# One recurrent block on one core: last batch's x fetched early, seven rows in round one, z fetched two blocks later, last values summed on TensorE, last stores in pieces

## The chip, the cores and the metric

The kernel runs on one core of one Trainium2 chip, in float32 throughout. The metric is the device time of one execution in microseconds (us). The engines are called PE (TensorE, matmuls), DVE (VectorE), ACT (ScalarE), POOL (GpSimd) and SP (SyncE, which here only issues DMAs). Each runs its own list of instructions in order and waits for the others through semaphores. DMAs are issued from a queue of SP, POOL or ACT.

## What is computed

For x of 8 batches of 1024 tokens of 256 features:

```
xn = layernorm(x)
s  = attention(xn)          # per token: 4 heads against 4 heads, softmax over heads
                            # heads and tokens swapped and reshaped, then Wo
z  = xn + experts(xn)       # Sinkhorn routing over 8 experts, the best 2 of each token
out = x + s * silu(z)
```

An expert is relu(x wg) * (x wp), times wo, for 512 hidden features. The attention is among the heads of one token, so its score is a 4x4 matrix for each token. The swap before Wo means that a row of s takes its parts from several tokens of the same batch: the s of a batch is complete only when all its tokens are.

## The kernel before

**Blocks.** A block (`blk`) is 4 tiles of 128 tokens, half a batch; there are 16. Normalised rows go to `xn_d` in DRAM, transposed ones to `xT_d`; `z_d` begins as a copy of `xn_d`.

**Attention as a generator.** `attention` (L866) yields after each small step, so that other loops can mix its steps with their own. For each tile `score` computes queries and keys (PE, L702) and their dot products (DVE, L715). Some blocks later `values_of` (L836) runs `value` (L766) for each tile. It computes the values times Wo, `u`, with four strips of 32 columns side by side on PE (`pu`, L785), adds a bias on DVE (L792), and sums over heads with the softmax weights `sc`. There are two forms of that sum. With `beside_experts[0]` set, DVE weighs (16 operations into `w`, L804 and L808), and PE puts the four head rows in place (`po_s`, L812, with an identity strip). Otherwise DVE builds a weighted identity, `mixer` (one operation, L773), and PE does the whole sum (`po_s`, L817). The weighing form yields once more. ACT copies the result to `s_out` (L824). After four tiles `values_of` stores `s_out` to `s_d` in the swapped order (L848) and marks the batch `attended`. For the last batch it keeps `s_out` in SBUF (`attended_rows`), since its two blocks can be finished in the swapped order of rows.

**Experts.** Of 71 possible groups of 256 (token, expert) pairs, the first 68 (`SURE`) always run; three more stand behind a branch (L1203) that this input doesn't take. A group is gathered, transposed (`ptr_g`, L933), multiplied by wg and wp (`pg`, `pp`, L945) and by wo (`po`, L961), scaled on ACT (L971) and added into `z_d` by two indirect DMAs of POOL (L974). The loop at L1192 takes an attention step after each of six steps of an expert. SP fetches the weights two groups ahead (L919).

**Finish.** When the last group has been added, the tail begins. For each block, `fetch_sums` (L1037) loads z from `z_d` into one of `SUMS` = 9 buffers, `fetch_other` (L1010) loads x and s into one of `AHEAD` = 8 pairs of buffers, and `finish` (L1052) does silu on ACT (L1059), the product with s and the sum with x on DVE (L1060, L1061), and the store from POOL (L1066; for the last batch four stores in swapped rows, L1064). Three pairs are loaded early, in the loop of experts (steps 96, 192 and 288), five when the scores are done and their buffers are free. The nine z loads come with the tail. In the tail each `finish` has four steps of attention ahead of it and the fetches of later blocks behind it: x and s of block `blk + 8`, then z of `blk + 9`. A fetch waits until the buffer's previous user is done: x and s for the sum of an earlier block on DVE, z for an earlier block's store. On SP's queue all later fetches stand behind a waiting one.

**Order.** The program's framework places instructions on each engine by its own estimate of times, so the order on PE, DVE and ACT isn't the order of the program text; DMAs of one queue stay close to it.

Of the kernel before, what the change touches and what calls it, by code (L numbers as in the profile page):

```python
# [9 lines left out]
F32 = mybir.dt.float32  # L10
AF = mybir.ActivationFunctionType
ALU = mybir.AluOpType
# [4 lines left out]
P = 128  # L17
# [13 lines left out]
def recurrent_kernel(  # L31
# [20 lines left out]
    nc = tc.nc  # L52
    B, S, D = x.shape
    H = phase.shape[0]
# [5 lines left out]
    J = P // R  # L60
    NT = S // P
    T = B * NT
    TB = 4
# [7 lines left out]
    SURE = N - 3  # L71
# [18 lines left out]
    def rows_of(a, b: int, first: int):  # L90

        return a[b * S + first * P : b * S + (first + TB) * P].rearrange(
            "(t p) d -> p t d", p=P
        )

    def block_of(a, blk: int):

        return a[blk * TB * P : (blk + 1) * TB * P].rearrange("(p t) d -> p (t d)", t=TB)
# [6 lines left out]
    n = 1  # L105
# [58 lines left out]
    s_d = dram.tile([B * S, D], F32, name="s_d")  # L164
# [601 lines left out]
    def value(tile_no: int, xT, t: int, sc, s_out):  # L766


        weigh = beside_experts[0]
        if not weigh:  # L770
            mixer = att.tile([P, H, H, J], F32, tag="mixer", name=f"mixer_{tile_no}")
            full = [P, H, H, J]
            nc.vector.tensor_tensor(  # L773
                mixer,
                onerow.unsqueeze(1).unsqueeze(1).to_broadcast(full),
                sc[:, t].rearrange("p (h g) -> p g h", h=H).unsqueeze(3).to_broadcast(full),
                ALU.mult,
            )
        u = att.tile([P, H * D], F32, tag="u", name=f"u_{tile_no}")
        for half in range(2):  # L780
            cols = slice(half * 512, (half + 1) * 512)
            pu = ps_tr.tile([P, 512], F32, tag="tr", name=f"pu_{tile_no}_{half}")
            for k in range(KD):
                for i in range(R):
                    nc.tensor.matmul(  # L785
                        pu[i * J : (i + 1) * J, :],
                        xT[:, t, k, i * J : (i + 1) * J],
                        w_vo[:, k, i, cols],
                        start=(k == 0),
                        stop=(k == KD - 1),  # L790
                    )
            nc.vector.tensor_tensor(  # L792
                u[:, cols], pu, b_vo.rearrange("p g d -> p (g d)")[:, cols], ALU.add
            )
            yield
        po = ps_out.tile([P, 512], F32, tag="out", name=f"po_s_{tile_no}")
        if weigh:

            w = att.tile([P, H, D], F32, tag="w", name=f"w_{tile_no}", bufs=1)
            for h in range(H):  # L800
                for g in range(H):
                    part, share = u[:, g * D : (g + 1) * D], sc[:, t, h * H + g : h * H + g + 1]
                    if g:
                        nc.vector.scalar_tensor_tensor(  # L804
                            w[:, h], part, share, w[:, h], ALU.mult, ALU.add
                        )
                    else:
                        nc.vector.tensor_scalar(w[:, h], part, share, None, ALU.mult)  # L808
            yield

            for h in reversed(range(H)):
                nc.tensor.matmul(  # L812
                    po[h * J : (h + 1) * J, :D], onerow, w[:, h], start=True, stop=True
                )
        else:
            for g in range(H):
                nc.tensor.matmul(  # L817
                    po[:, :D],
                    mixer[:, g].rearrange("p h r -> p (h r)"),
                    u[:, g * D : (g + 1) * D],  # L820
                    start=(g == 0),
                    stop=(g == H - 1),
                )
        nc.scalar.copy(s_out[:, t, :], po[:, :D])  # L824
        yield

    def fetch_turned(blk: int):
# [3 lines left out]
            xT.rearrange("p t k c -> p t (k c)"), xT_d[b][:, first : first + TB]  # L831
        )

    scored = {}

    def values_of(blk: int):  # L836

        b, first = blk * TB // NT, blk * TB % NT
        xT, sc = scored.pop(blk)
        s_out = att.tile([P, TB, D], F32, tag="s_out", name=f"s_out_{blk}")  # L840
        for t in range(TB):
            yield value(blk * TB + t, xT, t, sc, s_out)
        if b == B - 1:
            attended_rows[blk] = s_out
            return

        for h in range(H):
            nc.sync.dma_start(reshaped(s_d, blk, h), s_out[h * J : (h + 1) * J])  # L848
        if first + TB == NT:
            attended.add(b)  # L850
# [9 lines left out]
    def reshaped_rows(a, blk: int, h: int):  # L860

        b, first = blk * TB // NT, blk * TB % NT
        begin = b * S + (h * NT + first) * J
        return a[begin : begin + TB * J].rearrange("(t r) d -> r t d", r=J)
# [126 lines left out]
    def experts(begin: int, end: int):  # L991
        fetch_entries(begin)
        fetch_entries(begin + 1)
        fetch_expert(begin)
        for n in range(begin, end):
            if n + 2 < end:
                fetch_entries(n + 2)
            if n + 1 < end:
                fetch_expert(n + 1)
            yield from expert(n)  # L1000
            if n > begin:
                yield from late.pop(0)
        yield from late.pop(0)
# [1 line left out]

    AHEAD, SUMS = 8, 9

    def fetch_other(blk: int):  # L1010
        b, first = blk * TB // NT, blk * TB % NT
        slot, name = blk % AHEAD, f"fo_{blk}"
        if slot < 3:
            both = fin.tile([P, 2, TB, D], F32, tag="fo", name=name, bufs=3)
            xt, st = both[:, 0], both[:, 1]
        elif slot < 5:
            both = att.tile([P, 2, TB, D], F32, tag="qk", name=name)
            xt, st = both[:, 0], both[:, 1]
        elif slot < 6:
            xt, st = (att.tile([P, TB, D], F32, tag="kx", name=f"{name}_{n}") for n in range(2))  # L1020
        else:
            if slot == 6:
                four = queries.tile([P, 2, 2, TB, D], F32, tag="w_qk", name=name)
                for n in range(2):
                    other[blk + n] = four[:, n, 0], four[:, n, 1]
            xt, st = other[blk]
        if b == B - 1:
            for h in range(H):
                nc.sync.dma_start(xt[h * J : (h + 1) * J], reshaped_rows(x_rows, blk, h))
        else:  # L1030
            while b not in attended:
                run(att_gen, 1)
            nc.sync.dma_start(xt, rows_of(x_rows, b, first))
            nc.sync.dma_start(st.rearrange("p t d -> p (t d)"), block_of(s_d, blk))
        other[blk] = xt, st

    def fetch_sums(blk: int):  # L1037
# [12 lines left out]
    other, sums, attended_rows = {}, {}, {}  # L1050

    def finish(blk: int):  # L1052
        b, first = blk * TB // NT, blk * TB % NT
        z, (xt, st) = sums.pop(blk), other.pop(blk)
        if b == B - 1:
            while blk not in attended_rows:
                run(att_gen, 1)
            st = attended_rows[blk]
        nc.scalar.activation(z, z, AF.Silu)  # L1059
        nc.vector.tensor_tensor(z, z, st, ALU.mult)  # L1060
        nc.vector.tensor_tensor(z, z, xt, ALU.add)  # L1061
        if b == B - 1:
            for h in range(H):
                nc.gpsimd.dma_start(reshaped_rows(out_rows, blk, h), z[h * J : (h + 1) * J])  # L1064
        else:
            nc.gpsimd.dma_start(rows_of(out_rows, b, first), z)  # L1066


    def run(gen, n=None):
        done = 0  # L1070
        while (n is None or done < n) and next(gen, StopIteration) is not StopIteration:
            done += 1

    turned_rows, x_tiles, moments, all_scored = {}, {}, {}, []
    xT_tiles, newest, attended, stored, beside_experts = {}, {}, set(), [], [False]
    x_rows, out_rows = (a.rearrange("b s d -> (b s) d") for a in (x, out))
    att_gen = attention()
# [13 lines left out]
    n = TB  # L1091
# [97 lines left out]
    beside_experts[0] = True  # L1189
    held = nc.values_load(first_spare[:1, :1], min_val=0, max_val=E)  # L1190
    early = iter(range(AHEAD))
    for n, _ in enumerate(experts(0, SURE)):  # L1192
        run(att_gen, 1 if n % 3 or all_scored else 2)

        if n in (96, 192, 288):
            with tc.issue_after(issued[-1].ins):
                fetch_other(next(early))
    while not all_scored:
        run(att_gen, 1)
    for blk in early:  # L1200
# [6 lines left out]
    for blk in range(SUMS):  # L1207
        fetch_sums(blk)
    for blk in range(T // TB):
        run(att_gen, 4)  # L1210
        finish(blk)
        if blk + AHEAD < T // TB:
            fetch_other(blk + AHEAD)
        if blk + SUMS < T // TB:
            fetch_sums(blk + SUMS)
    run(att_gen)


# [33 lines left out]
```

## Time and profile before

| what | us |
|---|---|
| median of three runs (1683.54 to 1684.25) | 1683.59 |
| the profiled execution's own time | 1682.64 |
| its span in the trace | 1680.8 |
| PE busy | 1621.0 (96%) |
| DVE busy | 1201.8 (72%) |
| POOL busy | 635.3 (38%) |
| ACT busy | 427.5 (25%) |
| last expert's `po` ends | 1599.96 |
| its scatter-add lands, first z fetch issued | 1607.84, 1607.91 |
| PE's last `po_s` ends | 1667.09 |

The profile is of one execution. In a line of a timeline or chain stand the start in us, the duration in us, the engine, the line of the kernel, the operation, and `out<-in` by the program's names; in brackets the idle time before it and what ended it. A window line gives the busy time of each engine between two instants. `fz` is a block's z, `fo` the buffers of x and s. A float32 matmul shows as two records, so `po_s` of one tile is eight records.

### The profile page before, as it was taken

The numbers are of one execution on the slowest core, as the hardware profiler recorded it, in microseconds if no ns is written. First come the engines' busy times: TensorE is split into PE (matmuls) and PEld (weight loads), VectorE is DVE, ScalarE is ACT, GpSimd is POOL, SyncE is SP. The second block draws the span as 40 slices with busy tenths as digits, with TensorE's granted clock in tenths as the row PEclk, the third lists the DMA queues.
The fourth block names the chain that finished last, engine by engine and source line by source line (L and its number), as shares of the span: only waits on it lengthen the run. The fifth ranks groups of instructions, "written<-read, shape, count | busy, mean of one in ns | idle before, by whom it ended". The sixth has DMA issues, their size and how long they took to land.

```text
span 1680.8 us, 22808 instructions
## 1 busy us (share of the span) xinstructions
PE 1621.0 (96%) x7669; PEld 997.0 (59%) x7669; DVE 1201.8 (72%) x3689; ACT 427.5 (25%) x807; POOL 635.3 (38%) x599
## 2 busy tenths in 40 slices
PE   6888899999999999999999999999999999999986
PEld 4454344445666666666666666666666666767632
DVE  7779999997676757666566576675766756655767
ACT  4732122222222222222222222212222222222131
POOL 0311756574343433433533343334323433342212
PEclk9999999999999999999999999999999999999998
DMA  8993112123544544634544545445455445454489
GB/s 295 404 359 117 55 59 63 58 68 95 141 110 122 151 105 134 166 102 137 139 110 132 154 130 143 107 129 142 111 150 138 117 123 141 123 132 140 139 267 333
DMA packets 149175, 245.37 MB, mean 146 GB/s; under 512 B 15480, under 2 KB 93600, under 8 KB 148928
## 3 DMA queue, kind: packets, MB, share of 16 engines
q1 hardware_dynamic: 105648, 162.32, 29.5%
q0 software_dynamic: 41376, 77.38, 19.9%
q10 hardware_dynamic: 2032, 4.20, 0.7%
q8 instruction: 62, 1.02, 0.3%
q14 instruction: 57, 0.47, 0.1%
HBM read 176.85 MB, written 75.37 MB: 150 GB/s over the span
## 4 chain that ended last, share of the span: by engine, by line
PE 81%; DVE 11%; DMA 2%; issue 1%; ACT 1%; POOL 0%; SPq 0%; POOLq 0%; DVEq 0%; ACTq 0%
PE py L702 25%; PE po L961 13%; PE pg L945 12%; PE pp L945 12%; PE pu L785 12%; DVE junk L715 4%; PE po_s L817 3%; DVE kx L740 2%; PE ptr_g L933 2%; DVE w L804 2%; DMA fz<-z_d 1%; PE po_s L812 1%; DVE u L792 1%; DVE hid L954 1%; DVE w L808 0%
## 5 line engine op out<-in xcount | busy, mean ns | idle before, releaser
L974 POOL DMA_INDIRECT z_d<-y,row x136 | 232.8, 1712 | 668.9 <-ACT y L971 648.4
L702 PE MATMUL py<-w_qk,xTa 128*128 128x512 f32 x1024 | 476.0, 599 | 4.7 <-ACT qk L709 4.5
L715 DVE CUSTOM_DVE_ANT_0 junk<-qk,kx,lg 128x256 f32<-128x256 f32 x768 | 323.1, 478 | 0.2
L715 DVE CUSTOM_DVE_ANT_0 junk<-qk,lg 128x256 f32<-128x256 f32 x256 | 113.6, 480 | 265.6 <-ACT qk L709 265.4
L702 PEld LDWEIGHTS py<-w_qk,xTa 128*128 128x128 f32 x1024 | 189.6, 191 | 191.1 <-issue 175.8
L709 ACT COPY qk<-py 128x512 f32<-128x512 f32 x256 | 149.9, 586 | 466.3 <-PE py L702 442.8
L945 PE MATMUL pg<-xgT,wg 128*128 128x256 f32 x1088 | 264.3, 385 | 0.2
L945 PE MATMUL pp<-xgT,wp 128*128 128x256 f32 x1088 | 260.6, 381 | 0.3 <-DVE hid L954 0.3
L785 PE MATMUL pu<-w_vo,xTa 128*32 128x512 f32 x2048 | 258.6, 599 | 1.8 <-DVE u L792 1.1
L961 PE MATMUL po<-wd,hid 128*128 128x256 f32 x1088 | 257.7, 382 | 0.0
L945 PEld LDWEIGHTS pg<-xgT,wg 128*128 128x128 f32 x1088 | 201.9, 190 | 84.1 <-issue 41.5
L961 PEld LDWEIGHTS po<-wd,hid 128*128 128x128 f32 x1088 | 203.2, 190 | 68.1 <-issue 44.1
L740 DVE TENSOR_TENSOR kx<-qk,mixrow 128x1024 f32<-128x1024 f32 (+1 forms) x256 | 233.6, 950 | 0.0
L945 PEld LDWEIGHTS pp<-xgT,wp 128*128 128x128 f32 x1088 | 204.4, 190 | 39.0 <-ACT hid L953 7.5
L954 DVE TENSOR_TENSOR hid<-pp,hid 128x512 f32<-128x512 f32 x136 | 93.0, 684 | 137.8 <-PE pp L945 137.8
L804 DVE SCALAR_TENSOR_TENSOR w<-u,sc,w 128x256 f32<-128x256 f32 x444 | 185.8, 476 | 1.0
L682 POOL DMA_INDIRECT list_d<-entries,place x128 | 143.8, 1124 | 109.6 <-DVE place L679 74.9
L908 POOL DMA_INDIRECT xg<-xn_d,row x136 | 151.0, 1110 | 52.6 <-issue 40.9
L953 ACT ACTIVATE hid<-pg 128x512 f32<-128x512 f32 x136 | 81.2, 597 | 297.1 <-PE pg L945 288.3
L785 PEld LDWEIGHTS pu<-w_vo,xTa 128*32 128x32 f32 x2048 | 58.8, 109 | 136.6 <-issue 125.6
L971 ACT ACTIVATE y<-po,entry 128x256 f32<-128x256 f32 x136 | 57.2, 471 | 255.9 <-PE po L961 254.7
L792 DVE TENSOR_TENSOR u<-pu,b_vo 128x512 f32<-128x512 f32 x128 | 86.1, 683 | 27.5 <-PE pu L785 27.2
(214 smaller groups left out, 971.1 us busy)
## 6 DMA issues: line engine op xcount, KB each, us to landing
wg<-in_L_ffn_wg_dram SPq DMA_DIRECT2D x68, 512.0 KB, 3.7
wp<-in_L_ffn_wp_dram SPq DMA_DIRECT2D x68, 512.0 KB, 4.3
wd<-in_L_ffn_wo_dram SPq DMA_DIRECT2D x68, 512.0 KB, 3.8
list_d<-empty POOLq DMA_DIRECT2D x1, 9088.0 KB
x<-in_L_attn_x_dram SPq DMA_DIRECT2D x16, 512.0 KB, 8.8
xn_d<-x POOLq DMA_DIRECT2D x16, 512.0 KB
s_d<-s_out SPq DMA_DIRECT2D x56, 128.0 KB, 2.8
fo<-in_L_attn_x_dram SPq DMA_DIRECT2D x14, 512.0 KB, 4.7
```

Of the source, the lines that this page charges most:

```text
L682: put = nc.gpsimd.indirect_dma_start(list_d, bass.IndirectOffsetOnAxis(ap=piece[:, c : c + 1], axis=0), entries[:, at * 2 : at * 2 + LE], ...
L702: newest["score"] = nc.tensor.matmul(py, xT[:, t, k], w[:, k, cols], start=(k == 0), stop=(k == KD - 1),)
L709: nc.scalar.copy(flat[:, cols], py)
L715: newest["dot"] = nc.vector.tensor_tensor_reduce(junk, qk[:, 0, h], k, 1.0 / math.sqrt(D), lg[:, tile_no, E + at : E + at + 1], ALU.mult, ...
L740: nc.vector.tensor_tensor(kx[:, :w], k, mixrow[:, at : at + w].unsqueeze(2).to_broadcast([P, w, 2, D]), ALU.mult,)
L785: nc.tensor.matmul(pu[i * J : (i + 1) * J, :], xT[:, t, k, i * J : (i + 1) * J], w_vo[:, k, i, cols], start=(k == 0), stop=(k == KD - 1),)
L804: nc.vector.scalar_tensor_tensor(w[:, h], part, share, w[:, h], ALU.mult, ALU.add)
L908: nc.gpsimd.indirect_dma_start(xg[:, m], None, xn_d, bass.IndirectOffsetOnAxis(ap=row[:, m : m + 1], axis=0),)
L945: nc.tensor.matmul(dst[:, f], w[:, k, at : at + P], xgT[:, k], start=(k == 0), stop=(k == KD - 1),)
L954: nc.vector.tensor_tensor(h, pp, h, ALU.mult)
L961: nc.tensor.matmul(po[:, m], hid[:, f, m * P : (m + 1) * P], wd[:, f], start=(f == 0), stop=(f == KF - 1),)
L974: add = nc.gpsimd.indirect_dma_start(z_d, bass.IndirectOffsetOnAxis(ap=row[:, m : m + 1], axis=0), y[:, m], None, compute_op=ALU.add,)
```

## The change

- `AHEAD` is 7 instead of 8: round one loads seven pairs of x and s. The `fo` buffers of `fin` are two instead of three; in the room of the third stands `fl`, which holds x of the last two blocks.
- At step 96 of the experts the x of blocks 14 and 15 is fetched into `fl`, in swapped rows (eight DMAs of 128 KB). At 192 and 288 blocks 0 and 1 are fetched. Blocks 14 and 15 take no part in later rounds.
- In the tail z of block `blk + 7` is fetched behind `finish(blk)` from `blk` = 2 on, instead of `blk + 9` from 0 on.
- `beside_experts[0]` is cleared for the last 12 steps of the experts, so the values there take the mixer form.
- The first `finish` has eight steps of attention ahead of it instead of four.
- The last batch is finished in pieces: rows 0 and 1, then 2 and 3 of block 14; rows 0 and 1, then 2, then 3 of block 15. Each piece waits only for its own tiles, which `value` records in `valued`. Each of the four stores of a piece is issued from SP, POOL, SP and ACT in turn.

```diff
@@ value, values_of
         nc.scalar.copy(s_out[:, t, :], po[:, :D])
+        valued.add(tile_no)
         yield
...
-    AHEAD, SUMS = 8, 9
+    AHEAD, SUMS = 7, 9
@@ fetch_other
-        slot, name = blk % AHEAD, f"fo_{blk}"
+        if b == B - 1:
+            if first == 0:
+                both = fin.tile([P, 2, TB, D], F32, tag="fl", name=f"fo_{blk}", bufs=1)
+                for n in range(2):
+                    other[blk + n] = both[:, n], None
+            for h in range(H):
+                nc.sync.dma_start(
+                    other[blk][0][h * J : (h + 1) * J], reshaped_rows(x_rows, blk, h)
+                )
+            return
+        slot, name = blk % AHEAD + 1, f"fo_{blk}"
         if slot < 3:
-            both = fin.tile([P, 2, TB, D], F32, tag="fo", name=name, bufs=3)
+            both = fin.tile([P, 2, TB, D], F32, tag="fo", name=name, bufs=2)
@@ finish
+        ends = (2, 3, 4) if first else (2, 4)
+        for begin, end in zip((0, *ends), ends):
+            while blk * TB + end - 1 not in valued:
+                run(att_gen, 1)
+            piece = z[:, begin:end]
+            nc.vector.tensor_tensor(piece, piece, attended_rows[blk][:, begin:end], ALU.mult)
+            nc.vector.tensor_tensor(piece, piece, xt[:, begin:end], ALU.add)
             for h in range(H):
-                nc.gpsimd.dma_start(reshaped_rows(out_rows, blk, h), z[h * J : (h + 1) * J])
...
+                queue = (nc.sync, nc.gpsimd, nc.sync, nc.scalar)[h]
+                queue.dma_start(
+                    reshaped_rows(out_rows, blk, h)[:, begin:end], piece[h * J : (h + 1) * J]
+                )
@@ the loops
+    last_two = range(T // TB - 2, T // TB)
     for n, _ in enumerate(experts(0, SURE)):
+
+        beside_experts[0] = n < 6 * SURE - 12
         run(att_gen, 1 if n % 3 or all_scored else 2)
 
         if n in (96, 192, 288):
             with tc.issue_after(issued[-1].ins):
-                fetch_other(next(early))
+                for blk in last_two if n == 96 else (next(early),):
+                    fetch_other(blk)
...
     for blk in range(T // TB):
-        run(att_gen, 4)
+        run(att_gen, 4 if blk else 8)
         finish(blk)
-        if blk + AHEAD < T // TB:
+        if blk + AHEAD < last_two[0]:
             fetch_other(blk + AHEAD)
-        if blk + SUMS < T // TB:
-            fetch_sums(blk + SUMS)
+
+        if 0 <= blk - 2 < T // TB - SUMS:
+            fetch_sums(blk - 2 + SUMS)
```

More of the change, by code (lines that the diff above doesn't have):

```diff
@@ L832, in fetch_turned @@
         )
-    scored = {}
+    scored, valued = {}, set()
     def values_of(blk: int):
@@ L840, in values_of @@
         s_out = att.tile([P, TB, D], F32, tag="s_out", name=f"s_out_{blk}")
+        if b == B - 1:
+            attended_rows[blk] = s_out
         for t in range(TB):
@@ L843, in values_of @@
         if b == B - 1:
-            attended_rows[blk] = s_out
             return
@@ L1003, in experts @@
         yield from late.pop(0)
-    AHEAD, SUMS = 8, 9
+    AHEAD, SUMS = 7, 9
     def fetch_other(blk: int):
         b, first = blk * TB // NT, blk * TB % NT
-        slot, name = blk % AHEAD, f"fo_{blk}"
+        if b == B - 1:
+            if first == 0:
[8 more added lines that the diff above has]
+        slot, name = blk % AHEAD + 1, f"fo_{blk}"
         if slot < 3:
-            both = fin.tile([P, 2, TB, D], F32, tag="fo", name=name, bufs=3)
+            both = fin.tile([P, 2, TB, D], F32, tag="fo", name=name, bufs=2)
             xt, st = both[:, 0], both[:, 1]
@@ L1026, in fetch_other @@
             xt, st = other[blk]
[L1027 to L1034, printed above, removed]
+        while b not in attended:
+            run(att_gen, 1)
+        nc.sync.dma_start(xt, rows_of(x_rows, b, first))
+        nc.sync.dma_start(st.rearrange("p t d -> p (t d)"), block_of(s_d, blk))
         other[blk] = xt, st
@@ L1054, in finish @@
         z, (xt, st) = sums.pop(blk), other.pop(blk)
-        if b == B - 1:
-            while blk not in attended_rows:
-                run(att_gen, 1)
[L1058 to L1062, printed above, removed]
+        nc.scalar.activation(z, z, AF.Silu)
+        if b < B - 1:
+            nc.vector.tensor_tensor(z, z, st, ALU.mult)
+            nc.vector.tensor_tensor(z, z, xt, ALU.add)
+            nc.gpsimd.dma_start(rows_of(out_rows, b, first), z)
+            return
+        ends = (2, 3, 4) if first else (2, 4)
+        for begin, end in zip((0, *ends), ends):
+            while blk * TB + end - 1 not in valued:
+                run(att_gen, 1)
+            piece = z[:, begin:end]
+            nc.vector.tensor_tensor(piece, piece, attended_rows[blk][:, begin:end], ALU.mult)
+            nc.vector.tensor_tensor(piece, piece, xt[:, begin:end], ALU.add)
             for h in range(H):
-                nc.gpsimd.dma_start(reshaped_rows(out_rows, blk, h), z[h * J : (h + 1) * J])
-        else:
-            nc.gpsimd.dma_start(rows_of(out_rows, b, first), z)
+                queue = (nc.sync, nc.gpsimd, nc.sync, nc.scalar)[h]
+                queue.dma_start(
+                    reshaped_rows(out_rows, blk, h)[:, begin:end], piece[h * J : (h + 1) * J]
+                )
     def run(gen, n=None):
```

## The prediction, made before the changed kernel was run

> **What bounds the kernel now.** I read the page first: PE is busy 96% of the span, so whatever PE does before the last expert is on the path. The change touches almost nothing before the last two experts, so I then cut the end of the span into windows.
>
> ```profile
> 1575.00:1600.00 25.00, 24.77 (x150) 14.33 (x142) 16.96 (x40) 3.37 (x7) 6.38 (x4) 1.00 0.20 27
> 1600.00:1625.00 25.00, 18.90 (x130) 6.69 (x131) 14.35 (x22) 10.45 (x14) 4.76 (x4) 0.93 0.74 251
> 1625.00:1650.00 25.00, 25.00 (x162) 9.23 (x158) 21.23 (x24) 6.01 (x9) 4.52 (x6) 1.00 1.01 367
> 1650.00:1681.00 31.00, 17.09 (x106) 6.49 (x98) 21.40 (x22) 5.04 (x7) 8.90 (x14) 0.82 0.90 308
> ```
>
> Columns: PE, PEld, DVE, ACT, POOL busy, then granted clock, DMA share, GB/s. Until 1600 PE is full and the DMA nearly idle; from 1625 both are full. So two things can set the end: PE's last attention values, and the bytes of the tail. The chain of waits shows what starts the tail, and the timeline when PE gets going in it.
>
> ```profile
> 1596.30 3.67 PE po L961 x16
> ...
> 1600.79 7.06 DMA z_d<-y,row
> ...
> 1609.42 5.96 DMA fz<-z_d
> 1615.38 0.02 issue
> 1615.40 1.22 DVE fz L1060
> ...
> 1617.67 0.69 DVE u L792
> 1618.36 0.14 issue
> 1618.50 2.00 PE po_s L817 x4
> ```
>
> The last expert's output matmul ends at 1599.96; its scatter-add lands at 1607.84; only then may z be read (SP waits for it and issues its first z fetch at 1607.91). VectorE, in order, stands at block 0's product until 1614.26, and the u of the next value tile is behind it. PE waits for that u until 1618.50, then runs without a gap to 1667.09. I letter the 12 tiles left after all scores A to L (block 13: A to D, 14: E to H, 15: I to L); before, A and B are finished beside experts and C straddles the end.
>
> The end of the program:
>
> ```profile
> 1665.07 2.02 PE L817 MATMUL po_s<-u,mixer 128*128 128x256 f32 x8
> ...
> 1667.12 0.37 ACT L824 COPY s_out<-po_s 128x256 f32<-128x256 f32 x1 [4.18 <-PE po_s L817]
> ...
> 1670.17 1.06 ACT L1059 ACTIVATE fz<-fz 128x1024 f32<-128x1024 f32 x1 [1.72 <-DMA fz<-z_d]
> ...
> 1673.13 1.22 DVE L1061 TENSOR_TENSOR fz<-fz,fo 128x1024 f32<-128x1024 f32 x1 [0.64 <-DMA fo<-in_L_attn_x_dram]
> 1674.64 2.18 POOL L1064 DMA_DIRECT2D out_dram<-fz x4 [1.17 <-DVE fz L1061]
> ```
>
> The last loads (z 15, then x 15) come 3 and 6 us after PE is done; four stores then take 2.18 us to issue, and the span ends 3.98 us after that.
>
> **The change, part by part**, made against the profiled execution (span 1680.8, its own time 1682.64, the three runs' median 1683.59, so 0.95 is added at the end). The order of the instructions on each engine I took from both built kernels.
>
> *Last values beside experts on TensorE.* The last 12 steps (two experts) now use the mixer form. A mixer tile needs four steps of the generator, the weighing form five, so A, B and C all fit in front of the tail. Per tile, VectorE loses 16 weighing operations (12 at 0.476, 4 at about 0.33: 7 us) and gains one of 0.68. PE loses the four-strip sum (0.57) and gains the mixer sum (2.02 for 8 records). Where VectorE held PE here was only 0.77 us (1575.94 to 1576.71); the rest of this stretch is PE work. New order from 1575.94, with durations of the same rows: po_s A 2.12, transposes 0.44, a lone pu strip 1.05, pg 1.92, pp 1.73, pu 1.85, pg 1.92, pp 1.73, pu 1.88, po half 1.92, po_s B 2.02, po half 1.73, pu 1.85, po half 1.93, pu 1.85, po half 1.93. Sum 27.87, so the last expert ends at 1603.81 instead of 1599.96: **+3.85**. No wait for VectorE is left to win back, and SP's next step, the first z fetch, waits for exactly this. Scatter (7.88 from matmul to landing) and the first product move with it: 1611.7 and 1618.1. Bounds: +2.5 if some pu strip overlaps po_s, +4.6 if the 0.77 wait recurs; I take the sum.
>
> *VectorE's order in the tail.* The next u (E) is now behind two products instead of two products and a sum. ScalarE's order costs a little back, since the second silu is behind a copy of 0.37. So 2.5 after the first product's start instead of 3.41: u at 1620.6, PE restarts at 1621.4, which is **+2.9**.
>
> PE's work from there was 48.6 (1618.50 to 1667.09). It has the same tiles E to L, with one difference: between two halves of a sum PE puts in either one pu strip or four. One strip makes a tile 6.66 us (1625.93 to 1632.59), four make it 5.83 (1639.25 to 1645.08). Before, E and H have four; after, only E. **+0.85**: PE ends at 1670.85.
>
> The clock: PE's gap in front of E was 3.53 us, and the granted clock fell to 0.64 and 0.51 in the next 4 us. The first sum and strips took 2.00 and 1.73 instead of 1.06 and 1.00, so 1.7 us are already in the 48.6. After, D and E's pu are done by about 1615.7, so the gap is about 5.7. The Trainium skill (TensorE: Matmul & The Clock Gate, Part 1: The HAM clock gate) speaks against it: an idle window of about 3.4 us halves the clock, and the free-running window makes the cold time vary from run to run. By the row the new gap costs nothing extra; by the rule up to another window at half rate, an estimated 1.7. I take the row, 0, and keep -1.7 to +1.7.
>
> *x of the last batch early, seven rows in round one, z two blocks later.* Bytes don't change: before, the tail loads x of eight blocks and s of six; after, seven of each, because the last x takes the room of one pair. With 16 blocks of z, 16 of output and 0.5 MB of s stores it is 24.6 MB in both, about 64 us at the 385 GB/s of these windows. The eight early x pieces and 128 KB stores of s stand ahead of one owner read and one wg load near 671 us. Before, that wg is issued at 682.98 for an expert that starts at 693.48 and lands in 3.7, so some 6.8 us of slack cover about 2 us of moved issues: 0; without cover 2. Moving z behind the x and s fetches lets SP run ahead instead of waiting (it waited up to 7.4 for an output before). SP's new order is z 0 to 8, the s stores of block 13, x and s of 7, 8 and 9, then z 9, and from there a pair and a z in turn. The s stores wait for D's copy, now behind silu 0 (1618.5), and hold up only block 7's pair, which waits for block 0's sum near 1622 anyway. Each later pair waits for a sum on VectorE and holds the z behind it; by these sums z 15 is issued near 1660 and lands by about 1668, before it is used. So the loads leave the path, and the 3 to 6 us after PE's end become VectorE's.
>
> *The end.* In the new order two whole blocks are behind the last u, and silu 13 is behind the last s_out copy. From PE's end at 1670.85: last u done 1669.7; block 12's product and sum to 1672.05; copy 0.37 and silu 13 to 1672.35; block 13 to 1674.9; block 14 in four 128x512 operations at 0.61 apart (taken from the 0.68 mixer row) to 1677.4. Here is a new wait: ScalarE now issues two of block 14's stores, and they are in front of silu 15. The second waits for block 14's last sum, so silu 15 starts at about 1677.85 (an ACT-issued load took 0.37 to 0.48 at the start of the trace) and ends at 1678.95. Block 15's six operations take 2.65, to 1681.6. SP issues its two last stores by 1682.3 (0.35 each), and 3.9 more as before: 1686.2. Without the queue on ScalarE it would be 1.5 less.
>
> *Stores in pieces.* They replace 1.22 of last sum and 2.18 of issue by 0.38 and 0.7. The Trainium skill (DMA: Bandwidth & Descriptors, Bandwidth) says that transfers under 64 KB are descriptor-dominated; here they are 64 and 32 KB. By the rule the last 0.5 MB would drain slower, by perhaps 1 us as an estimate. But in the last six microseconds the DMA share was only about 0.36, and 128 KB stores of s landed in 2.8, so I take 0, with +1 as upper bound.
>
> Sum: 3.85 - 0.95 + 0.85 = +3.75 at PE's end, and 15.35 instead of 13.7 behind it: +5.4. Span 1686.2, median **1689.0**.
>
> **Rivals.**
>
> 1. *The tail is set by its bytes, and the end chain is shorter than I make it.* For it: DMA share 1.0 from 1625 on. The start moves by 3.85, 64 us of transfers from 1613 end near 1677, and then the short store, about 4.5: 1681.7, so +0.9, **1684.5**. This is no measurable change (a measurement of this kernel tells about 0.2%, 3.4 us). Against it: the same saturation hid under PE's unbroken run to 1667.
>
> 2. *Faster: bytes again, but with no later start.* If the mixer sums fit where PE's records only look busy, transfers start near 1609.4 as before. With SP running ahead they keep some 400 GB/s (the best five-microsecond windows show 406 to 409), so 24.6 MB end at 1670.9, and 4.5 more give 1675.4: -5.4, **1678.2**. It decides once the start moves by less than 2 us. Against it: PE is busy for 24.77 of 25 us there, and the operations behind its chain add up without a gap.
>
> 3. *The early reordering doesn't stay hidden*, near 671 us: +2 more, **1691**.
>
> **How the numbers follow.** My forecast 0.52, the reordering or a long cold clock beside it 0.08, rival 1 0.27, rival 2 0.13. Faster by over 0.2%: 0.13; slower by over 0.2%: 0.60; within: 0.27. The forecast's own range is 1686.5 to 1691.5 (start +2.5 to +4.6, clock up to 1.7, ScalarE's queue 1.5). To leave out no more than 2 in 10 the range goes down into rival 1: 1682.0 to 1692.0.
>
> **What would show it.** Right: the last expert's po ends near 1603.8 and the first z fetch is issued near 1611.7; PE restarts near 1621.4 and ends near 1671; silu 15 starts after block 14's last sum, with its z landed long before. Wrong: a first z fetch before 1609; a DMA-bound end, with z 15 landing after 1672; or PE ending before 1668.

## The result and the profile after

The changed kernel took 1686.86 us (median of 20 runs, 1684.50 to 1691.04), the kernel before 1683.57 (median of 20 runs beside them, 1678.82 to 1686.01). The ratio is 1.0017, 95% interval [1.0010, 1.0024]: slower by 0.17%, some 3 us. That is real, by the interval, but just inside the 0.2% that I had called no change. The profiled execution has a span of 1685.4 us (its own time 1687.13), against 1680.8 (1682.64) before. The difference of the two profiles, 4.5 us, is larger than that of the medians, 3.3, because the profiled run of before fell 0.93 under its median and this one 0.27 over its own.

The whole difference is made after 1560: the anchor that I use for every trace below, the first transpose (`ptr_g`) of the last expert but one, starts at 1559.86 before and at 1559.61 after. The same windows as before, with the same columns (PE, PEld, DVE, ACT, POOL busy, granted clock, DMA share, GB/s):

```profile
1575.00:1600.00 25.00, 25.00 (x144) 15.37 (x140) 5.54 (x8) 3.37 (x7) 5.81 (x4) 1.00 0.15 18
1600.00:1625.00 25.00, 18.41 (x114) 8.32 (x107) 9.37 (x11) 8.55 (x11) 4.76 (x4) 0.86 0.67 210
1625.00:1650.00 25.00, 25.00 (x154) 9.05 (x152) 20.93 (x24) 5.30 (x8) 3.76 (x5) 1.00 1.05 401
1650.00:1681.00 31.00, 20.36 (x124) 7.79 (x122) 24.76 (x31) 7.32 (x10) 6.87 (x10) 0.87 0.88 302
```

In the first window DVE is relieved (5.54 instead of 16.96) and PE is no faster for it: it was full and is full. In the second window fewer bytes move (210 GB/s instead of 251), and the third makes up most of it (401 instead of 367). The timeline of the changed kernel around the start of the tail:

```profile
1600.95 1.99 PE L963 MATMUL po<-wd,hid 128*128 128x256 f32 x8
1602.78 1.89 PE L817 MATMUL po_s<-u,mixer 128*128 128x256 f32 x8
...
1610.97 4.33 SPq L1057 DMA_DIRECT2D fz<-z_d  x9
...
1617.23 2.44 DVE L1066 TENSOR_TENSOR fz<-fz,fo 128x1024 f32<-128x1024 f32 x2 [5.42 <-ACT fz L1064]
...
1619.59 0.68 DVE L792 TENSOR_TENSOR u<-pu,b_vo 128x512 f32<-128x512 f32 x1
...
1620.42 2.04 PE L817 MATMUL po_s<-u,mixer 128*128 128x256 f32 x4 [5.77 <-ACT fz L1064]
```

The last expert's `po` ends at 1602.94 (1600.95 + 1.99), 2.98 later than before; the first z is asked for at 1610.97, 3.06 later. DVE does two products, then the u that PE waits for, and PE starts again at 1620.42, 1.92 later. PE is named as waiting for ACT's `fz`, but the chain goes through DVE's u, which stands behind the two products, and these behind silu 0.

And its end:

```profile
1668.35 2.00 PE L817 MATMUL po_s<-u,mixer 128*128 128x256 f32 x8
...
1676.13 0.90 ACTq L1080 DMA_DIRECT2D out_dram<-fz  x2
...
1677.23 1.06 ACT L1064 ACTIVATE fz<-fz 128x1024 f32<-128x1024 f32 x1 [4.56 <-DVE fz L1077]
...
1680.65 0.42 DVE L1077 TENSOR_TENSOR fz<-fz,fo 128x256 f32<-128x256 f32 x1
```

The last sum of PE ends at 1670.35, 3.26 later than before. ACT's last silu starts only when ACT has issued its two stores of block 14; the second waits for DVE's last sum of that block. The last operation of DVE ends at 1681.07, the span 4.33 later.

### The profile page after: what moved, and what is told of

Its sections match the earlier page's. It is cut to its first block, busy times and chain, and to the rows that moved or that the text cites. A ratio compares the mean times of both kernels' runs of the same rounds, so it can differ in the third digit from the quotient of the medians.

```text
span 1685.4 us, 22788 instructions
## 1 busy us (share of the span) xinstructions
PE 1622.9 (96%) x7669; PEld 1000.3 (59%) x7669; DVE 1186.7 (70%) x3650; ACT 427.3 (25%) x807; POOL 636.0 (38%) x596
## 5 line engine op out<-in xcount | busy, mean ns | idle before, releaser
L804 DVE SCALAR_TENSOR_TENSOR w<-u,sc,w 128x256 f32<-128x256 f32 x408 | 170.7, 476 | 0.7
```

The lines of the kernel that those rows point to most:

```text
L804: nc.vector.scalar_tensor_tensor(w[:, h], part, share, w[:, h], ALU.mult, ALU.add)
```

## The experiments

No kernel here leaves out work; they only place it elsewhere. All ratios are to the kernel before, measured beside it on the same chip. Single runs of one kernel in one batch spread over 2 to 14 us, so a ratio tells about 0.1%, and one trace shows where time goes better than how much of it there is. In the traces I compare five distances from the anchor, in us:

| kernel | last po ends | first z issued | PE restarts | PE ends | span ends |
|---|---|---|---|---|---|
| before | 40.1 | 48.1 | 58.6 | 107.2 | 120.9 |
| after | 43.3 | 51.4 | 60.8 | 110.7 | 125.8 |
| after, weighing form (second run) | 40.1 | 48.2 | 58.0 | 108.3 | 123.3 |
| before, mixer form (second run) | 43.3 | 51.3 | 61.9 | 111.2 | 124.0 |
| 6 steps put off (further down) | 34.7 | 45.6 | 53.0 | 110.0 | 121.5 |
| 12 steps put off (further down) | 25.3 | 36.2 | 42.9 | 102.8 | 111.7 |

My theory: the time comes from the start, that is from the mixer sums of A, B and C on PE in front of the last expert's `po`; the reordered fetches and the pieces cost nothing or little. Rivals: the reordered tail costs, or the end chain does.

**The mixer form taken out of the changed kernel, and put alone into the kernel before.** Each was run in two batches.

```diff
@@ the loops, taken out of the changed kernel (first kernel), put into the one before (second)
     for n, _ in enumerate(experts(0, SURE)):
+        beside_experts[0] = n < 6 * SURE - 12
```

Without it in the changed kernel, the expectations of the two batches were:

> The changed kernel with one part undone: the last two experts' values take the weighing form again. Start theory (the mixer sums on TensorE make the last expert end some 3 us later, and the whole tail moves with it): the last expert's po ends 3 us earlier, PE's last po_s near 1667.5, and the median is 2.5 to 3.5 below the changed kernel, near 1684. End theory (the loss is made behind PE's end, by silu and stores in a new order): no more than 0.5 below it. Early theory (fetches moved near 671 us): no change.

> Repeat of the changed kernel with the weighing form, to narrow the interval: the theory of the start (the mixer sums beside experts are what costs) says within 0.08% of before; the rival (the reordered tail costs) says 0.1 to 0.25% above before.

With it alone in the kernel before:

> The kernel before with one part added: the last 12 expert steps take the mixer form. Start theory: the last expert's po ends 3 us later, and the median is 2.5 to 3.5 above before, near 1686.5. End theory and early theory: within 0.5 of before.

> Repeat of the kernel before with the mixer form in the last 12 expert steps only: theory of the start 0.1 to 0.25% above before; the rival within 0.08%.

Measured: without it 0.9995 [0.9986, 1.0004] and 1.0002 [0.9993, 1.0011]; with it alone 1.0010 [0.9999, 1.0020] and 1.0006 [0.9997, 1.0015]. So all other parts of the change together are worth nothing that can be measured, and the 0.17% goes when this one line goes. The line by itself shows about 0.08% (1.7 and 1.0 us, where I had expected 2.5 to 3.5), the mean of two values whose intervals both include no change; whether it costs less in the kernel before than in the changed one can't be told from these intervals. The table shows the first links of the mechanism: in both kernels that carry the line the last `po` ends at 43.3 us, in both that don't at 40.1, and the first z follows it by 8. Its last column doesn't show the whole effect in this one line: without the line the changed kernel's trace is still 2.4 longer than that of before, behind a PE end 1.1 later, though the medians show no difference. One trace of each can't settle 2 us. The timeline of the changed kernel without the line (second run):

```profile
1596.04 3.72 PE L963 MATMUL po<-wd,hid 128*128 128x256 f32 x16
...
1606.05 0.64 PE L812 MATMUL po_s<-w,onerow 128*32 128x256 f32 x8 [1.67 <-DVE w L804]
...
1607.81 4.79 SPq L1057 DMA_DIRECT2D fz<-z_d  x9
...
1617.68 1.10 PE L817 MATMUL po_s<-u,mixer 128*128 128x256 f32 x4 [2.91 <-DVE u L792]
```

The four-strip sum (0.64) is back where the mixer sum took 2 us, and z is asked for at 1607.81 again. The kernel before with the line (second run) has the late start:

```profile
1601.31 1.99 PE L961 MATMUL po<-wd,hid 128*128 128x256 f32 x8
...
1611.23 4.94 SPq L1048 DMA_DIRECT2D fz<-z_d  x9
```

**Only the fetches, and only the pieces,** put into the kernel before.

```diff
@@ only the fetches, in the kernel before: AHEAD, fetch_other and the loops as in the change
-    AHEAD, SUMS = 8, 9
+    AHEAD, SUMS = 7, 9
...
-        run(att_gen, 4)
+        run(att_gen, 4 if blk else 8)
```

> The kernel before with the fetch parts alone: last x ahead, seven rows, z two blocks later, eight steps ahead of the first finish; weighing form, last batch whole and stored from POOL. Start theory: within 1.5 of before, and the loads of the last blocks land long before they are used. Early theory: 3 above before. End theory: within 1.5, since neither pieces nor ScalarE stores are in it.

```diff
@@ only the pieces, in the kernel before: finish as in the change
+        ends = (2, 3, 4) if first else (2, 4)
+        for begin, end in zip((0, *ends), ends):
...
+                queue = (nc.sync, nc.gpsimd, nc.sync, nc.scalar)[h]
```

> The kernel before with the pieces alone: last batch multiplied, summed and stored in pieces from SP, POOL, SP and ACT. Start theory: between 2 below before (the last sum and the issue of stores are shorter by 2 us) and 1 below, since silu 15 now waits behind block 14's stores on ScalarE. End theory: 2 or more above before.

Measured: 1.0003 [0.9989, 1.0017] and 0.9999 [0.9987, 1.0010]. Neither gives or costs anything that a measurement here can tell. The interval of the pieces, about 2 us wide, is too wide to tell the prediction's estimate of 1 us for small stores from none. In the trace after, SP's stores of 64 KB landed in a median of 2.8 us and those of 32 KB in 2.0, the 128 KB stores of s in 2.8: no loss from their size shows.

**The stores on ACT's queue moved to POOL's**, in the changed kernel, which frees the last silu of the wait for block 14's sums.

```diff
@@ finish
-                queue = (nc.sync, nc.gpsimd, nc.sync, nc.scalar)[h]
+                queue = (nc.sync, nc.gpsimd, nc.sync, nc.gpsimd)[h]
```

> The changed kernel, but the stores that it issues from ScalarE are issued from POOL. Start theory: only silu 15 gets free of block 14's sums, 1 to 1.5 us below the changed kernel. End theory: 3 below it, near 1684. Early theory: no change.

Measured: 1.0013 [1.0004, 1.0022], not to be told from the changed kernel's 1.0017. Its timeline (this chip was slower before the tail, so the instants are some 16 us later):

```profile
1689.38 1.06 ACT L1064 ACTIVATE fz<-fz 128x1024 f32<-128x1024 f32 x1 [0.69 <-DMA fz<-z_d]
...
1692.67 5.21 POOL L1080 DMA_DIRECT2D out_dram<-fz  x10 [1.37 <-DVE fz L1077]
...
1694.91 0.42 DVE L1077 TENSOR_TENSOR fz<-fz,fo 128x256 f32<-128x256 f32 x1
```

The last silu now waits only for its z (0.69 instead of 4.56), and from PE's end to DVE's last sum there are 8.96 us instead of 10.72: 1.76 won, as I had said (1.5). But POOL issues ten stores one after the other at 0.52 each and is done 2.55 after the last sum, and the span ends 6.07 after it instead of 4.33: 1.74 lost. The wait moved from one in-order queue to the next.

**Both removed**, mixer line and ACT's stores (the two diffs above together):

> The changed kernel with the weighing form for all values beside experts and no store on ScalarE. Start theory: the two gains add up, 4 below the changed kernel, near 1683 and so 0 to 1 below before. End theory: 3 below the changed kernel, all of it from the stores.

Measured: 0.9994 [0.9985, 1.0003]. Again no more than before.

**PE's gap closed.** The kernel with both removed, with 14 steps of attention ahead of the first finish, and with the products of the first nine blocks held behind the u of those steps, so that DVE serves PE first. The diff is to that kernel; `newest["u"]` is the latest u operation of `value`.

```diff
@@ finish
-            nc.vector.tensor_tensor(z, z, st, ALU.mult)
+            with tc.issue_after(newest["u_first"].ins) if blk < 9 else nullcontext():
+                nc.vector.tensor_tensor(z, z, st, ALU.mult)
@@ the loops
-        run(att_gen, 4 if blk else 8)
+        run(att_gen, 4 if blk else 14)
+        newest.setdefault("u_first", newest["u"])
```

> As the kernel with weighing form and no store on ScalarE, but the first finish stands behind more attention steps (14), and the products of the first nine blocks are kept behind the u of the tiles of those steps on VectorE. If PE's restart (held by a u behind the first products) sets the end, then PE's gap of some 5 us and its cold clock go, PE ends 5 us earlier, and the median is 2 to 4 lower than with the weighing form and no store on ScalarE. If the bytes of the tail set the end, nothing is gained: within 1.

Measured: 0.9999 [0.9991, 1.0008]. PE ran on into the tail without the gap or a slow clock and ended 101.4 us after the anchor, 5.8 earlier than before, and none of it reached the end. The profiled run was the slowest of its eleven, 1.9 over their median. Its windows, and ACT's timeline:

```profile
1600.00:1625.00 25.00, 22.43 (x170) 8.59 (x166) 13.40 (x21) 12.67 (x16) 3.19 (x3) 1.00 0.67 222
1625.00:1650.00 25.00, 25.00 (x154) 9.21 (x150) 21.46 (x25) 3.12 (x6) 5.35 (x7) 1.00 0.98 366
```

```profile
1668.56 1.06 ACT L1064 ACTIVATE fz<-fz 128x1024 f32<-128x1024 f32 x1 [6.53 <-DMA fz<-z_d]
1672.42 1.06 ACT L1064 ACTIVATE fz<-fz 128x1024 f32<-128x1024 f32 x1 [2.81 <-DMA fz<-z_d]
1673.82 1.06 ACT L1064 ACTIVATE fz<-fz 128x1024 f32<-128x1024 f32 x1 [0.34 <-DMA fz<-z_d]
```

The last three silus wait for their z. The products that were held back release their buffers later: SP waits 16.7 us in all for DVE before it can fetch an x, 9.8 in the kernel without the hold. Fewer bytes move early (222 and 366 GB/s, where the kernel without the hold moves 250 and 392), and at the end it is the transfers that are late. PE's end and the bytes are two limits of about the same length here; easing one shows the other.

**The start moved the other way.** If later mixer sums cost time because they delay z, then taking PE's attention work away from in front of the last `po` must win time, as long as both limits move. Two kernels skip the attention steps beside the last 6 and the last 12 steps of the experts; the tail does that work instead. They have the weighing form, the hold of the last experiment with 12 steps instead of 14, and the fourth store of block 14 on SP instead of ACT; block 15's stays on ACT. The diff is to the changed kernel.

```diff
@@ finish, besides the hold above
+                queue = (nc.sync, nc.gpsimd, nc.sync, nc.scalar if first else nc.sync)[h]
@@ the loops
-        beside_experts[0] = n < 6 * SURE - 12
-        run(att_gen, 1 if n % 3 or all_scored else 2)
+        if n < 6 * SURE - 12:      # or - 6
+            run(att_gen, 1 if n % 3 or all_scored else 2)
...
+        run(att_gen, 4 if blk else 12)
```

> The changed kernel with the weighing form beside the last experts, no store of block 14 on ACT, and no attention step beside the last 6 expert steps (one expert); that work is done in the tail. If the instant at which the first z fetch is issued sets the end (theory of the start, now with the opposite sign), the last expert's po and the first z fetch come some 4 to 6 us earlier than before and the time is 0.15 to 0.35% below before. If PE's total work sets the end (rival), the work put off comes back behind the start and the time stays within 0.1% of before.

> The same with no attention step beside the last 12 expert steps. Theory of the start: po and first z fetch 8 to 12 us earlier, time 0.3 to 0.6% below before, as long as PE's work put off still fits in the 65 us that the bytes take; rival (PE's total work): within 0.1% of before, or slower where PE waits for the experts' own chain without attention to fill it.

Measured: 0.9994 [0.9985, 1.0004] with 6, no gain where I had expected 0.15 to 0.35%, and **0.9929 [0.9916, 0.9941]** with 12, 1672.71 us against 1684.27 beside it: 0.71% faster than before, more than the 0.3 to 0.6% expected. Windows of the kernel with 12, and then PE and SP in its timeline:

```profile
1575.00:1600.00 25.00, 23.97 (x152) 14.64 (x154) 5.53 (x8) 2.87 (x6) 7.20 (x5) 1.00 0.40 71
1600.00:1625.00 25.00, 23.16 (x149) 8.79 (x138) 19.82 (x23) 11.99 (x15) 3.63 (x5) 1.00 1.03 389
1625.00:1650.00 25.00, 25.00 (x157) 9.02 (x155) 20.39 (x23) 5.62 (x8) 4.48 (x7) 1.00 1.04 402
```

```profile
1580.27 5.78 PE L963 MATMUL po<-wd,hid 128*128 128x256 f32 x26
1587.08 3.64 PE L785 MATMUL pu<-w_vo,xTa 128*32 128x512 f32 x32 [1.03 <-ACTq L1223]
...
1596.89 5.46 SPq L1057 DMA_DIRECT2D fz<-z_d  x9
...
1603.59 1.99 PE L817 MATMUL po_s<-u,mixer 128*128 128x256 f32 x8 [1.84 <-ACT s_out L824]
...
1661.55 2.01 PE L817 MATMUL po_s<-u,mixer 128*128 128x256 f32 x8
```

The last `po` ends at 1586.05, 13.9 earlier, and the first z is asked for at 1596.89, 11.0 earlier (14.8 and 11.9 by the anchor, which lies 0.9 later in this trace). The 2.9 between the two are lost on POOL: the last expert's y is done at 1586.97, but POOL waits until 1589.10 before it starts the scatter-add at 1589.79. The second scatter-add of the expert before lands at 1589.07, by the last of the sixteen completion steps that the trace records for it, so this is what POOL waits for. The work that was put off fills the time in which PE used to stand: its waits from there on are 1.03 and 1.84, the clock stays at 1.00, and it ends at 1663.56, 3.5 earlier. The DMA is full from 1600 on (389 GB/s instead of 251), and the last four silus don't wait for their z: from PE's end to DVE's last sum there are 4.16 us (6.56 with 6 steps, 10.72 in the changed kernel). 3.5 earlier at PE, and 8.8 instead of 13.7 behind it, make the 8.4 us between the two spans. The medians lie 11.56 apart: this profiled run was 1.42 over its median and that of before 0.93 under its own, and before was 0.70 slower on this chip.

With 6 steps the z came only 2.4 earlier by the anchor (at 1603.85), and this gain was spent at once:

```profile
1603.85 4.83 SPq L1057 DMA_DIRECT2D fz<-z_d  x9
...
1611.23 3.78 PE L817 MATMUL po_s<-u,mixer 128*128 128x256 f32 x8 [5.01 <-ACT s_out L824]
1614.95 4.67 PE L785 MATMUL pu<-w_vo,xTa 128*32 128x512 f32 x32
```

PE waits 5.01 for a copy of ACT, since that copy stands on ACT behind two silus that wait for z (the chain of waits has them at 1608.92 and the copy at 1610.83); its clock falls, and the two groups take 8.45 instead of 5.65 (2.01 and 3.64 in the kernel with 12). PE ends at 1668.20, by the anchor 2.8 later than before.

**Further: 18 steps.** The chain of the kernel with 12 goes through PE alone from 1603 to 1663, so I asked whether PE's total work is the limit now.

```diff
-        if n < 6 * SURE - 12:
+        if n < 6 * SURE - 18:
```

> As the kernel with 12 steps put off, but with no attention step beside the last 18 expert steps. In the trace of that kernel the chain of waits runs through PE alone from the first value tiles of the tail to its last sum. If PE's total work is now what sets the end, the time is the same as with 12 steps (0.6 to 0.8% below before), although z is fetched another 4 to 6 us earlier. If the start and the bytes still set it, it falls by another 0.25 to 0.35%.

Measured: 0.9970 [0.9957, 0.9983]: faster than before, but worse than with 12, which neither theory had said. The timeline of PE and of ACT (another slow chip):

```profile
1612.19 3.75 PE L817 MATMUL po_s<-u,mixer 128*128 128x256 f32 x8 [6.44 <-DVE scm L757]
...
1621.33 1.96 PE L817 MATMUL po_s<-u,mixer 128*128 128x256 f32 x8 [1.73 <-DVE u L792]
```

```profile
1615.26 1.28 ACT L1064 ACT_TABLE_LOAD   x1 [13.35 <-DMA fz<-z_d]
1616.55 1.06 ACT L1064 ACTIVATE fz<-fz 128x1024 f32<-128x1024 f32 x1
1617.63 1.28 ACT L759 ACT_TABLE_LOAD   x1
1618.92 0.26 ACT L759 ACTIVATE sc<-sc 128x64 f32<-128x64 f32 x1
1619.19 1.28 ACT L1064 ACT_TABLE_LOAD   x1
```

Now the last scores too fall into the tail. Their softmax needs ACT's exponential (L759), which stands behind silu 0, which waits for z 0; DVE first works for 9.5 us on those scores (1601.94 to 1611.43), and later waits 6.31 for the exponential; PE waits 6.44 and 1.73, and the first sum and strips run at the slow clock (3.75 and 3.73). So of the three amounts 12 is the best: enough to cover the way of z, and not so much that work with a long chain of its own comes behind z.

What these runs leave open: putting 12 steps off was not tried without the hold on DVE's products, nor with block 14's fourth store elsewhere, so how the 0.71% divides between these was not measured. The hold with 14 steps ahead gave nothing, and the kernels with 6 and 12 steps differ in nothing but the steps put off, so the step from no gain to 0.71% is theirs.

## Why the prediction was right, step by step

The forecast was 1689.0 with 1682.0 to 1692.0 around it; it came to 1686.86. The number alone decides little: it lies 2.14 under my forecast and 2.36 over rival 1's 1684.5, and it fell among the changes within 0.2%, to which I had given 0.27, not among those slower by more, with 0.60. That the forecast is the nearer of the two is luck, by a margin smaller than the spread of the runs. What speaks for the mechanism is its steps, which came out so:

| step | predicted | trace after |
|---|---|---|
| last expert's `po` ends | 1603.81 | 1602.94 |
| first z issued | 1611.7 | 1610.97 |
| first product on DVE | 1618.1 | 1617.23 |
| PE restarts | 1621.4 | 1620.42 |
| PE ends | 1670.85 | 1670.35 |
| silu 15 starts | 1677.85 | 1677.23 |
| DVE's last sum ends | 1681.6 | 1681.07 |
| span | 1686.2 | 1685.4 |

- **The start** (+3.85) was 0.87 too long: the stretch from `po_s` A began 0.36 earlier than the 1575.94 of before that I counted from, and its 16 pieces took 27.36 us, not 27.87. The sum of rows was right to 2%, but the shift itself, a difference of two such sums, was 2.98 (3.2 by the anchor). Taking the line out of the changed kernel takes the measured slowdown away; put alone into the kernel before it showed about half of it. So the line is needed for the effect, and that it makes the whole of it is not shown. Of the 4.6 us between the two spans 1.9 are there when PE restarts, 1.3 come in PE's work from there, and 1.3 behind its end.
- **The order of DVE in the tail** (-0.95) was right: two products and then u. Restart minus first product is 3.19, predicted 3.3.
- **The lost four-strip split** (+0.85): PE's work from the restart was 49.93 us instead of 48.6, predicted 49.45. The other 0.48 is the clock, where I had chosen 0. In the changed kernel's chain of waits the first half sum, strips and half sum took 2.04, 1.87 and 1.41 us, which at full speed take 1.06, 1.00 and 1.06: 2.2 lost, against 1.7 before. The prediction's rule of the clock gate, with its upper end of 1.7 more, had the right sign, and the row the better size.
- **The reordered early part** cost nothing: the anchor lies 0.25 us earlier than before.
- **The end** (15.35 behind PE's end) was 15.05. The wait of silu 15 for ACT's stores was there in full, but "without the queue on ScalarE it would be 1.5 less" did not come true with POOL in its place: the 1.76 won came back as 1.74 of issue.
- **z 15** was to land by 1668, and was later. SP's eight z fetches of the last batch, with the DMA full, took 14.87 us to issue; for 10.4 of these SP waited for loads issued earlier to land. The chain of waits after has these two steps:

```profile
1652.12 14.54 DMA fz<-z_d
1666.68 3.92 DMA fz<-z_d
```

SP's last fetch goes out at 1666.68, when the first has landed. The chain ends its way at 1670.60, but that is the twelfth of the sixteen completion steps that the trace records for it; the last comes at 1671.72. That is 1.4 after PE's end, and just before ACT has done silu 14 (1672.67). With ACT's stores gone (on POOL) silu 15 did wait for its z, until 3.0 us after PE's end. In the changed kernel it was held until 1677.23 in any case, so the late z cost nothing.
- **From span to median.** I added 0.95 for the place of the profiled run under its median. The changed kernel's profiled run lay 0.27 over its own, so of the 2.14 that the forecast was too high, 0.8 is the span, 1.2 this offset, and 0.1 what lies around the span. The run-to-run spread was of the size of the effect.

Rival 1 (the bytes set the end) was closer than I made it: z 15 was complete 1.4 us after PE's end, so that transfers and PE's chain were nearly level, though the wait for ACT's stores came behind both and set the time. Closing PE's gap won 5.8 us on PE and nothing at the end. Rival 2 (no later start) fell with the first z at 1610.97. Rival 3 (the early reordering) fell with the anchor. What I had not seen is that the start could be used the other way: the same argument, turned round, gives 0.71%.

## What to carry to other kernels

When a tail starts with a long dependent way (here matmul, scatter, load, silu, product: 18.5 us from the last `po` to PE's restart before), ask what stands in front of its first link on the busiest engine, and put off whatever the tail can do instead: work put off fills the wait, work moved in front lengthens it. The amount matters: here 6 steps gave nothing that could be measured, 12 gave 0.71% and 18 gave 0.30%. Relieving an engine that isn't the limit (7 us of DVE per tile here) with 1.5 us more on the one that is can cost time: here the last expert ended 3 us later. And where two limits lie close together, a gain on one alone shows nothing; move both, and watch which in-order queue the next wait goes to.

## What the hardware showed unexpectedly

- PE's clock fell after shorter waits than the 3.53 us of before too. After waits of 2.91 and 2.65 us PE started at full speed (1.10 and 1.13 for half a sum), and about a microsecond later the clock was at 0.50: the next strip took 1.85 and 1.92 instead of 1.04. After a wait of 2.75 in the kernel with only the fetches it did not fall at all. The Trainium skill (TensorE: Matmul & The Clock Gate, Part 1: The HAM clock gate) names an idle window of about 3.4 us, free-running; that the outcome varies agrees, that 2.65 us can be enough is this case's addition.
- A single `pu` strip costs PE as much as four side by side: 0.97 us (2 records) against 1.00 (8 records). In the kernel with 12 steps put off a tile with lone strips takes 6.66 us (by its chain) and PE sets the time from 1603 to 1663; a better split was not tried.
- A store of 32 or 64 KB takes 0.50 to 0.56 us to issue on POOL, 0.32 to 0.47 on SP and 0.33 to 0.44 on ACT.
- Each change between exponential and silu on ACT cost a table load of 1.28 us; with 18 steps put off there are three of them within 5.2 us, on the path.
